# One pass over the edge tiles in layer 0's messages, with two accumulating products a tile

## The chip, the core and the metric

The kernel runs on one core of a Trainium2 chip. Its engines are TensorE (PE; its weight loads are shown as PEld), VectorE (DVE), ScalarE (ACT), GpSimd (POOL) and SyncE (SP), each with its own queue of instructions, and 16 DMA engines. The metric is the device time of one execution in microseconds (us), as the median of several runs.

## What is computed

Two blocks of a network on a graph: 6250 nodes with 256 features, 100000 edges sorted by `dst`. The change lies in the first layer, a graph convolution with symmetric normalisation (cut to what matters; self-loops are added to the edges):

```python
deg = segment_sum(ew_sl, row_sl)
dinv = where(deg > 0, rsqrt(deg), 0.0)
norm = dinv[row_sl] * ew_sl * dinv[col_sl]
xw = h6_all @ W
msgs = xw[col_sl] * norm[:, None]
h7 = segment_sum(msgs, row_sl) + b
h = relu(h7 @ W1 + b1)
out = h @ W2 + b2
```

Here `row` is `src` and `col` is `dst`: each edge takes the row of its `dst` node, times its weight, and adds it to its `src` node. After this layer come a mixture of 8 experts, a relational graph layer with 8 relations over the same edges (gathered by `src`, summed by `dst`), and a mixture of 6 experts. The data are float32.

## The kernel before, in words

Nodes are cut into NT = 49 blocks of 128. The edges, in the order of `dst`, are C_ = 782 tiles of 128 edges. They are written as records (dst, src, weight, src*8+type) to `edge_table` in HBM. If the edges are found not to be sorted by block, the branch at L207 reorders them first; it is not taken with these data.

**Tiles by block.** A tile of edges can straddle two blocks of `dst`. `tile_list` (L241) makes a list in which such a tile stands once for each block that it touches: T = C_ + NT - 1 = 830 entries, padded to TL = 832, in Q = 7 columns of 128. An indirect DMA on POOL (L315) gathers the edge table in that order into `M`. `dloc` (L330) is the edge's dst relative to the entry's block; `mine` (L333, L334) marks the edges of the entry that belong to that block; `srcm` (L335) is src+1 for those and 0 for the others. `dloc` goes to HBM as `lane_rows` (L337). `to_edges` (L340) turns four of these arrays by PE transposes so that an entry's 128 edges lie on the partitions: `srcT`, `ewT`, `dlocT`, `idxT`. `blkd` holds each entry's block. The pool "edges", in which all this lies, is closed at L354, and the pool "keys" takes its side of the memory.

**Keys and degrees (L532 to L698).** From `srcT` each edge entry gets a place in the order by `src`: comparisons against 49 blocks (`eq`, L545), counts (`pcnt`), a running sum, and for each block two pairs of products and a predicated copy into `pos` (L597 to L604), between which `x_times_w` produces the layer's product xw tile by tile into HBM. `at` (L612) is the place; edges that are not the entry's own have none. Then the weighted degree: over chunks of DCH = 32 columns, DVE builds one comparison (`ohl`, L663) and three products (`we`, L671), and PE accumulates one small product for each column (L678). `dinv` is known at L697. These loops run over all 832 columns.

**Messages (L699 to L771).** xw is loaded into `acc` (49 blocks of 256 columns and one of zeros), and ACT scales each block by `dinv` (L729). Then for each group of 8 entries: SP loads `lane_rows` broadcast over the partitions (L714, three groups ahead), DVE compares it with the partition's number to make eight selection matrices `sT` (L751), and copies the src number into the end of the message (L753); and for each entry PE multiplies the matrix with the block of `acc` named by a register (L756), ACT scales by the weight (L759), and POOL scatters the 128 rows of 260 floats to their places in `msgs` in HBM (L762). Rows without a place are skipped. `sT` has three buffers, `msg` four groups, and `psum_mm` four banks, one for each `px`. SP also loads x into X in five pieces (L743, L745), to which DVE adds b2 (L749).

```python
ps = psum_mm(f"px{t0 + j}")
nc.tensor.matmul(
    ps[:, :D], sT[:, j, :], acc[:, bass.ds(blocks[j] * D, D)], start=True, stop=True
)
```

**Sums (L774 to L797)** read `msgs` back in the order of `src` and add each tile into `acc`. Layer 1 (`layer1`, L1366, with `aggregate`, L799) uses `dlocT`, `idxT` and `blkd`, and stands in an if with an else (L1413 to L1416).

The code is written in a framework that sets the waits between the engines and orders the instructions between two branches by their dependences, not strictly as written.

Of the kernel before, what the change touches and what calls it, by code (L numbers as in the profile page):

```python
# [20 lines left out]
D = 256  # L21
E = 100000
NT = 49
# [8 lines left out]
TH = TL // 2  # L32
NOWHERE = 127 + 128 * 1024
# [6 lines left out]
DCH = 32  # L40
# [12 lines left out]
def gnn_ffn_kernel(ctx: ExitStack, tc: tile.TileContext, a, out):  # L53
# [221 lines left out]

    turn_i = sp.tile([128, Q * 128], I32, name="turn_i")
# [45 lines left out]

    Mf = M.bitcast(F32)
    dloc = sp.tile([128, Q, 128], F32, name="dloc")
    srcm = sp.tile([128, Q, 128], F32, name="srcm")
    idxf = sp.tile([128, Q, 128], F32, name="idxf")
    mine = sp.tile([128, Q, 128], F32, name="mine")
    dlocb = sp.tile([128, Q, 128], BF16, name="dlocb")
# [3 lines left out]
    nc.scalar.copy(dlocb, dloc)  # L332
    nc.vector.tensor_scalar(mine, dloc, 0.0, None, op0=OP.is_ge)  # L333
    nc.vector.scalar_tensor_tensor(mine, dloc, 128.0, mine, op0=OP.is_lt, op1=OP.mult)  # L334
    nc.vector.scalar_tensor_tensor(srcm, M[:, :, :, 1], 1.0, mine, op0=OP.add, op1=OP.mult)  # L335
    lane_rows = dram.tile([Q * 128, 128], BF16, name="lane_rows")
    nc.sync.dma_start(lane_rows.rearrange("(q p) e -> p q e", p=128), dlocb)  # L337


    def to_edges(name, pool, rows, dt):  # L340
        t = pool.tile([128, Q * 128], dt, name=name)
        for q0 in range(0, Q, 4):
            n = min(4, Q - q0)
            pt = psum_mm(f"p_{name}{q0}")
            for q in range(n):
                nc.tensor.transpose(pt[:, q * 128 : (q + 1) * 128], rows(q0 + q), ident)
            nc.scalar.copy(t[:, q0 * 128 : (q0 + n) * 128], pt[:, : n * 128])
        return t

    srcT = to_edges("srcT", g0p, lambda q: srcm[:, q], F32)  # L350
    ewT = to_edges("ewT", g0p, lambda q: Mf[:, q, :, 2], F32)
    dlocT = to_edges("dlocT", ed, lambda q: dloc[:, q], F32)
    idxT = to_edges("idxT", ed, lambda q: idxf[:, q], I32)
# [180 lines left out]
    srcT_i = kp.tile([128, TL], I32, name="srcT_i", tag="t1")  # L534
    nc.vector.tensor_scalar(srcT_i, srcT[:, :TL], -1.0, None, op0=OP.add)
    key_i = kp.tile([128, TL], I32, name="key_i", tag="t2")
    nc.vector.tensor_scalar(key_i, srcT_i, 7, None, op0=OP.arith_shift_right)
    hib = kp.tile([128, TL], BF16, name="hib")
    nc.vector.tensor_copy(hib, key_i)
    nc.vector.tensor_scalar(key_i, srcT_i, 127, None, op0=OP.bitwise_and)  # L540
    lob = kp.tile([128, TL], BF16, name="lob")
    nc.vector.tensor_copy(lob, key_i)
    eq = kp.tile([128, NT, TL], BF16, name="eq")
# [7 lines left out]
    for b in range(NT):  # L551
        for h in range(2):
            nc.tensor.matmul(
                pcnt[h][:NT, :TH],
                sel[:, NT - 1 - b : 2 * NT - 1 - b],
                eq[:, b, h * TH : (h + 1) * TH],
                start=(b == 0),
                stop=(b == NT - 1),
            )
    cnts = kp.tile([NT, TL], F32, name="cnts", tag="t1")  # L560
    for h in range(2):
        nc.scalar.copy(cnts[:, h * TH : (h + 1) * TH], pcnt[h][:NT, :TH])
    base = kp.tile([NT, TL], F32, name="base", tag="t3")
    one = ones[:NT, 0:1].to_broadcast([NT, TL])
    nc.vector.tensor_tensor_scan(base, one, cnts, 0.0, op0=OP.mult, op1=OP.add)
    tots = kp.tile([NT, 1], F32, name="tots")
    nc.vector.tensor_copy(tots, base[:, TL - 1 :])
# [12 lines left out]
    base_i = kp.tile([NT, TL], I32, name="base_i", tag="t2")  # L580
    nc.vector.scalar_tensor_tensor(base_i, base, start0, cnts, op0=OP.add, op1=OP.subtract)
    qr = kp.tile([64 + NT, TL], F16, name="qr")
    nc.vector.memset(qr, 0.0)
    half_i = kp.tile([NT, TL], I32, name="half_i", tag="t4")
# [10 lines left out]
    pos = kp.tile([128, TL], F32, name="pos", tag="t3")  # L595
    nc.vector.memset(pos, float(NOWHERE))
    for b in range(NT):  # L597
        for h in range(2):
            cs = slice(h * TH, (h + 1) * TH)
            pp = psum_mm(f"ppos{b}_{h}")  # L600
            nc.tensor.matmul(pp[:, :TH], beforeb, eq[:, b, cs], start=True, stop=False)
            nc.tensor.matmul(pp[:, :TH], selq[:, b : b + 1].to_broadcast([64 + NT, 128]), qr[:, cs], start=False, stop=True)
            nc.vector.copy_predicated(pos[:, cs], eq[:, b, cs].bitcast(U16), pp[:, :TH])
        next(xws, None)  # L604

    place = kp.tile([128, TL], I32, name="place", tag="t1")
    nc.vector.tensor_copy(place, pos)
    slot = kp.tile([128, TL], I32, name="slot", tag="t2")
    nc.vector.tensor_scalar(slot, place, 7, None, op0=OP.arith_shift_right)
    nc.vector.tensor_scalar(place, place, 127, None, op0=OP.bitwise_and)  # L610
    at = g0p.tile([128, TL], I32, name="at")
# [3 lines left out]
    past_s = kp.tile([NT, TL], F32, name="past_s", tag="t4")  # L615
# [32 lines left out]
    parts = kp.tile([128, 3, TL], BF16, name="parts")  # L648
    rest = kp.tile([128, TL], F32, name="rest", tag="t1")
    nc.vector.tensor_copy(parts[:, 0], ewT[:, :TL])  # L650
    nc.vector.tensor_sub(rest, ewT[:, :TL], parts[:, 0])
# [8 lines left out]
    for c0 in range(0, TL, DCH):  # L660
# [16 lines left out]
        for c in range(DCH):  # L677
# [5 lines left out]
                stop=(c0 + c == TL - 1),  # L683
# [24 lines left out]
    expand = ctx.enter_context(ExitStack())  # L708
    xp = expand.enter_context(tc.tile_pool(name="expand", bufs=3))

    def lanes_of(t0):

        rows = xp.tile([128, 8, 128], BF16, name=f"rows{t0}", tag="rows")
        nc.sync.dma_start(  # L714
            rows,
            lane_rows[t0 : t0 + 8, :].rearrange("(o t) e -> o t e", o=1).to_broadcast([128, 8, 128]),
        )
        return rows

# [14 lines left out]
    for t0 in range(0, TL, 8):  # L734
# [3 lines left out]
        if t0 + 24 < TL:  # L738
            ahead.append(lanes_of(t0 + 24))
# [733 lines left out]
```

## Time and profile before

| | us |
|---|---|
| median of 3 runs | 4283.4 (4282.7 to 4290.7) |
| the profiled execution | 4289.8 |
| its span, first to last instruction | 4288.1 |
| start to the last degree product | 0 to 384.6 |
| acc loaded and scaled | 386.3 to 414.4 |
| messages, first to last scatter | 416.5 to 1501.6 |
| sums, first read to the last product of the loop | 1503.2 to about 2000 |
| experts of layer 0, table of layer 1 | to 2943 |
| layer 1 with its experts | 2950 to the end |

```profile
span 4288.1 us, 48381 instructions
...
PE 3382.5 (79%) x12377; PEld 2237.3 (52%) x12377; DVE 1945.9 (45%) x5379; ACT 1016.3 (24%) x2275; POOL 2131.5 (50%) x2341
...
PE   2886555556555389997859959998789999999999
...
POOL 1000777777777755553740071003766666666640
PEclk9998777676776699998869979997889999999999
```

The last three rows cut the span into 40 slices of 107 us; a digit is the busy share in tenths, and for PEclk the share of its full clock that TensorE was granted. The messages are slices 5 to 14, counted from 1: POOL at 7, PE at 5 or 6, the clock at 6 or 7. A float32 product shows as two MATMUL rows.

### The profile page before, as it was taken

To read this page: it belongs to the slowest core of one execution; us is meant where nothing else is said; L and a number is where in the kernel's file an instruction comes from. 1 tells how busy PE (TensorE), PEld (TensorE's weight loads), DVE (VectorE), ACT (ScalarE), POOL (GpSimd) and SP (SyncE) were. 2 spreads that over 40 slices of the span, in tenths; PEclk is the share of its full clock that TensorE was granted. 3 is DMA by queue.
4 is the path that set the end of the run, shared out by engine and by line. 5 is a ranking of instruction groups with operands and counts; after the bars stand their busy time and mean duration, and the time that the engine had idled before them with its cause. 6 is when DMAs were issued, how large, how long until landed. Compare 5 with 4: busy or idle time off the path is not lost.

```text
span 4288.1 us, 48381 instructions
## 1 busy us (share of the span) xinstructions
PE 3382.5 (79%) x12377; PEld 2237.3 (52%) x12377; DVE 1945.9 (45%) x5379; ACT 1016.3 (24%) x2275; POOL 2131.5 (50%) x2341
## 2 busy tenths in 40 slices
PE   2886555556555389997859959998789999999999
PEld 1565444444444245554647724444556666666666
DVE  6686100000001078886743354333556566555552
ACT  3312333333333200000624411221111221212113
POOL 1000777777777755553740071003766666666640
PEclk9998777676776699998869979997889999999999
DMA  5514433333333266665233353333333333333320
GB/s 171 153 38 136 133 126 122 123 119 123 120 123 122 101 223 229 229 229 192 74 122 108 106 181 145 128 128 117 101 86 96 94 95 100 95 97 96 92 75 9
DMA packets 222105, 531.42 MB, mean 124 GB/s; under 512 B 44269, under 2 KB 128482, under 8 KB 201859
## 3 DMA queue, kind: packets, MB, share of 16 engines
q0 software_dynamic: 89648, 240.41, 17.6%
q1 hardware_dynamic: 105200, 209.11, 15.0%
q10 hardware_dynamic: 26976, 78.69, 5.3%
q8 instruction: 111, 1.82, 0.2%
q14 instruction: 170, 1.39, 0.1%
HBM read 317.07 MB, written 217.49 MB: 125 GB/s over the span
## 4 chain that ended last, share of the span: by engine, by line
PE 47%; DVE 6%; DMA 4%; POOL 3%; issue 3%; ACT 1%; DVEq 0%; SPq 0%; ACTq 0%; POOLq 0%
PE pa1a L820 7%; PE phx L1242 7%; PE pa L795 6%; PE ph_e1a L426 6%; PE py1a L899 5%; PE ph_e2a L426 5%; POOL m L793 2%; PE pf L1179 2%; PE pf L1195 2%; DMA y<-ys,ats 2%; DVE acc L797 2%; PE pt_fh L414 1%; DVE acc L822 1%; PE plo L1256 1%; PE pg L984 1%
## 5 line engine op out<-in xcount | busy, mean ns | idle before, releaser
L813 POOL DMA_INDIRECT g1a<-hx,idxT x830 | 800.8, 965 | 764.8 <-issue 399.1
L762 POOL DMA_INDIRECT msgs<-msg,at x830 | 832.4, 1003 | 598.9 <-DMA X<-in_x 346.2
L756 PE MATMUL px<-acc,sT 128*128 x1660 | 606.9, 544 | 475.5 <-ACT msg L759 442.6
L756 PEld LDWEIGHTS px<-acc,sT 128*128 128x128 f32 x1660 | 463.4, 286 | 618.3 <-ACT msg L759 482.4
L822 DVE TENSOR_TENSOR acc<-acc,pa1a 128x256 f32 x830 | 348.2, 420 | 392.8 <-PE pa1a L820 364.9
L759 ACT ACTIVATE msg<-px,ewT 128x256 f32<-128x256 f32 x830 | 357.6, 475 | 695.6 <-DMA msgs<-msg,at 566.4
L795 PE MATMUL pa<-g,m 128*128 128x256 f32 x1660 | 448.6, 419 | 84.4 <-DVE m L785 44.5
L820 PE MATMUL pa1a<-g1a,m1a 128*128 128x256 f32 x1660 | 480.2, 405 | 26.8 <-DMA g1a<-hx,idxT 12.3
L820 PEld LDWEIGHTS pa1a<-g1a,m1a 128*128 128x128 f32 x1660 | 318.3, 199 | 224.3 <-issue 147.8
L795 PEld LDWEIGHTS pa<-g,m 128*128 128x128 f32 x1660 | 250.7, 189 | 282.7 <-issue 115.8
L1242 PE MATMUL phx<-wr,xT 128*128 128x512 f32 x784 | 364.6, 619 | 36.0 <-DVE hx L1250 29.3
L797 DVE TENSOR_TENSOR acc<-acc,pa 128x256 f32 x830 | 348.4, 420 | 73.8 <-PE pa L795 5.9
L793 POOL TENSOR_SCALAR m<-lanes,key 128x128 f32<-128x128 f32 x414 | 263.8, 652 | 228.7 <-PE pa L795 205.7
L753 DVE COPY msg<-srcT 128x32 f32<-128x32 f32 x104 | 18.9, 183 | 696.2 <-DMA msgs<-msg,at 696.0
L899 PE MATMUL py1a<-w_L_ffn_expert_w,v2a 128*128 128x256 f32 x1176 | 284.1, 382 | 4.8 <-DVE acc L822 2.2
L426 PE MATMUL ph_e1a<-xT3a,w_L_ffn_expert_w 128*128 128x512 f32 (+2 forms) x672 | 284.8, 549 | 0.2 <-DVE acc L822 0.2
L426 PE MATMUL ph_e2a<-v1a,w_L_ffn_expert_w 128*128 128x512 f32 (+2 forms) x672 | 279.7, 542 | 2.6 <-DVE acc L822 2.2
L1242 PEld LDWEIGHTS phx<-wr,xT 128*128 128x128 f32 x784 | 152.3, 198 | 219.5 <-issue 181.9
L1219 POOL DMA_INDIRECT y<-ys,ats x98 | 96.7, 986 | 303.8 <-DMA w_L_ffn_expert_w<-in_L_ffn_expert_w 274.2
L899 PEld LDWEIGHTS py1a<-w_L_ffn_expert_w,v2a 128*128 128x128 f32 x1176 | 220.4, 190 | 43.8 <-ACT v2a L433 8.7
L433 ACT ACTIVATE v1a<-ph_e1a,cols 128x512 f32<-128x512 f32 (+2 forms) x168 | 106.5, 634 | 575.9 <-PE ph_e1a L426 575.8
L900 DVE SCALAR_TENSOR_TENSOR X<-py1a,C1a,X 128x256 f32<-128x256 f32 x294 | 139.2, 482 | 126.3 <-PE py1a L899 125.6
(606 smaller groups left out, 3756.6 us busy)
## 6 DMA issues: line engine op xcount, KB each, us to landing
g<-msgs SPq DMA_DIRECT2D x52, 1040.0 KB
g<-msgs ACTq DMA_DIRECT2D x52, 1040.0 KB, 4.9
hx<-hx SPq DMA_DIRECT2D x49, 1024.0 KB, 3.8
rows<-lane_rows SPq DMA_DIRECT2D x104, 256.0 KB, 3.6
fx<-xs SPq DMA_DIRECT2D x105, 128.0 KB, 2.0
ys<-fy ACTq DMA_DIRECT2D x105, 128.0 KB
msgs<-msg,at POOLq DMA_INDIRECT x830, 2.5
g1a<-hx,idxT POOLq DMA_INDIRECT x830, 2.8
```

What stands on the lines that cost most here:

```text
L426: nc.tensor.matmul(ps[:, :ncols], w[:, k, f * 128 : (f + 1) * 128], xT[:, k, :ncols], start=(k == 0), stop=(k == 1),)
L756: nc.tensor.matmul(ps[:, :D], sT[:, j, :], acc[:, bass.ds(blocks[j] * D, D)], start=True, stop=True)
L759: nc.scalar.activation(msg[:, j, :D], ps[:, :D], AF.Copy, scale=ewT[:, t0 + j : t0 + j + 1])
L762: ins = nc.gpsimd.indirect_dma_start(out=msgs, out_offset=bass.IndirectOffsetOnAxis(ap=at[:, t0 + j : t0 + j + 1], axis=0), in_=msg[:, j, ...
L793: nc.gpsimd.tensor_scalar(m[:, j], lanes, key[:, j : j + 1], None, op0=OP.is_equal)
L795: nc.tensor.matmul(ps[:, :D], m[:, j, :], g[:, j, :D], start=True, stop=True)
L797: nc.vector.tensor_add(here, here, ps[:, :D])
L813: nc.gpsimd.indirect_dma_start(out=g, out_offset=None, in_=table, in_offset=bass.IndirectOffsetOnAxis(ap=idxT[:, t0 + j : t0 + j + 1], axi ...
L820: nc.tensor.matmul(ps[:, :D], m[:, j, :], g, start=True, stop=True)
L822: nc.vector.tensor_add(here, here, ps[:, :D])
L899: nc.tensor.matmul(ps[:, :D], hT[:, k, j : j + 128], w[:, k, :], start=(k == 0), stop=(k == 1))
L1242: nc.tensor.matmul(ps, xT[:, k, :], wr[:, k, 2 * i : 2 * i + 2, :].rearrange("p r o -> p (r o)"), start=(k == 0), stop=(k == 1),)
```

## The change

The list of edge tiles that the messages use is now the natural one: each of the 782 tiles once (TN = 784 columns). What a tile needs beside its first block is taken from the block after it. A new table `Mn` is loaded without an indirect DMA; `lane` is the edge's dst relative to the tile's first block, 0 to 255 for an edge of the first two. Two comparisons per group of tiles make one selection matrix for each of the two blocks, and two products accumulate in PSUM. Two tiles share one PSUM bank, half each. Keys, places and degrees run over 784 columns instead of 832, and the degree chunks are 28 columns instead of 32. The gathered list stays for layer 1 (`dlocT`, `idxT`, `blkd`), and the places in `msgs` and the sums keep their 830 entries.

If any real edge lies beyond the second block (`far`), a flag is set, and a branch chooses another form of the loop, in which each tile's rows come by an indirect DMA from a copy of the scaled xw in HBM. The loop with the two products stands in its else.

```diff
+TN = (C_ + 7) // 8 * 8
+QN = (C_ + 127) // 128
+NH = TN // 2
-DCH = 32
+DCH = 28
...
+    nc.sync.dma_start(
+        Mn[:, : QN - 1].rearrange("p q e r -> p q (e r)"), table[:whole].rearrange("(q p) x -> p q x", p=128)
+    )
...
+    nc.vector.tensor_scalar(firstb_i, Mn[:, :, 0, 0], 7, None, op0=OP.arith_shift_right)
...
+    nc.vector.tensor_scalar(real, Mn[:, :, :, 0], float(NP), None, op0=OP.is_lt)
+    nc.vector.scalar_tensor_tensor(srcm, Mn[:, :, :, 1], 1.0, real, op0=OP.add, op1=OP.mult)
+    for q in range(QN):
+        nc.vector.tensor_scalar(lane[:, q], Mn[:, q, :, 0], firstn[:, q : q + 1], None, op0=OP.subtract)
+    nc.scalar.copy(laneb, lane)
...
+            nc.tensor.matmul(
+                pbn[:1, q * 128 : (q + 1) * 128], firstb[:, q0 + q : q0 + q + 1], ident, start=True, stop=True
+            )
...
+    nc.vector.tensor_mul(lane, lane, real)
+    nc.vector.tensor_reduce(far, lane, axis=AX.X, op=OP.max)
+    nc.vector.tensor_scalar(far, far, 256.0, None, op0=OP.is_ge)
...
-    nc.scalar.copy(dlocb, dloc)
-    nc.vector.tensor_scalar(mine, dloc, 0.0, None, op0=OP.is_ge)
-    nc.vector.scalar_tensor_tensor(mine, dloc, 128.0, mine, op0=OP.is_lt, op1=OP.mult)
-    nc.vector.scalar_tensor_tensor(srcm, M[:, :, :, 1], 1.0, mine, op0=OP.add, op1=OP.mult)
...
-    for t0 in range(0, TL, 8):
-        blocks = blocks_of(blkd, t0, [ENG.PE], NT)
+    def messages(tag, near):
...
+            for t0 in range(0, TN, 8):
+                n = min(8, C_ - t0)
...
-        sT = xp.tile([128, 8, 128], F32, name=f"sT{t0}", tag="sT")
-        nc.vector.tensor_scalar(sT, rows, part, None, op0=OP.is_equal)
+                if near:
+                    blocks = blocks_of(blkn, t0, [ENG.PE], NT - 1)
+                    sT = xp.tile([128, 2, 8, 128], F32, name=f"sT{tag}{t0}", tag="sT", bufs=2)
+                    for k in range(2):
+                        nc.vector.tensor_scalar(
+                            sT[:, k], rows, far_parts[:, k : k + 1], None, op0=OP.is_equal
+                        )
...
-            ps = psum_mm(f"px{t0 + j}")
-            nc.tensor.matmul(
-                ps[:, :D], sT[:, j, :], acc[:, bass.ds(blocks[j] * D, D)], start=True, stop=True
-            )
+                    if near:
+                        if j % 2 == 0:
+                            pair = psum_mm(f"px{tag}{t0 + j}")
+                        come = pair[:, j % 2 * D : (j % 2 + 1) * D]
+                        for k in range(2):
+                            nc.tensor.matmul(
+                                come,
+                                sT[:, k, j, :],
+                                acc[:, bass.ds(blocks[j] * D + k * D, D)],
+                                start=(k == 0),
+                                stop=(k == 1),
+                            )
+                    else:
+                        come = xp.tile([128, D], F32, name=f"come{tag}{t0 + j}", tag="come")
+                        nc.gpsimd.indirect_dma_start(
+                            out=come,
+                            out_offset=None,
+                            in_=xw,
+                            in_offset=bass.IndirectOffsetOnAxis(ap=to[:, j, 0:1], axis=0),
+                        )
...
+    nfar_v = nc.values_load(nfar[0:1, 0:1], min_val=0, max_val=128, skip_runtime_bounds_check_because="it is a count")
+    with tc.If(nfar_v > 0) as far_cmp:
+        messages("f", False)
+    with far_cmp.Else():
+        messages("n", True)
```

## The prediction

> **What bounds the kernel now.** I read the page's table of costliest groups first: the change sits in the message loop (L733 to L771), and three rows of that table are its engines.
>
> ```profile
> L762 POOL DMA_INDIRECT msgs<-msg,at x830 | 832.4, 1003 | 598.9 <-DMA X<-in_x 346.2
> ...
> L756 PE MATMUL px<-acc,sT 128*128 x1660 | 606.9, 544 | 475.5 <-ACT msg L759 442.6
> ...
> L759 ACT ACTIVATE msg<-px,ewT 128x256 f32<-128x256 f32 x830 | 357.6, 475 | 695.6 <-DMA msgs<-msg,at 566.4
> ```
>
> The columns after the bar are busy us, mean ns of one, idle us before and who ended it. ACT waits for scatters to land, PE waits for ACT: both run behind POOL. Then the timeline, at the start of the loop and in its middle (start, duration, idle before in brackets):
>
> ```profile
> 414.54 3.75 PE L756 MATMUL px<-acc,sT 128*128 x8 [30.01 <-DMA X<-in_x]
> 415.77 0.47 ACT L759 ACTIVATE msg<-px,ewT 128x256 f32<-128x256 f32 x1 [1.33 <-PE px L756]
> 416.52 1.02 POOL L762 DMA_INDIRECT msgs<-msg,at  x1 [346.20 <-DMA X<-in_x]
> ...
> 902.56 0.47 ACT L759 ACTIVATE msg<-px,ewT 128x256 f32<-128x256 f32 x1 [0.38 <-PE px L756]
> 903.41 0.47 ACT L759 ACTIVATE msg<-px,ewT 128x256 f32<-128x256 f32 x1 [0.38 <-PE px L756]
> ...
> 905.36 0.98 POOL L762 DMA_INDIRECT msgs<-msg,at  x1 [0.30 <-issue]
> 906.64 0.98 POOL L762 DMA_INDIRECT msgs<-msg,at  x1 [0.30 <-DMA msgs<-msg,at]
> ...
> 910.51 1.10 POOL L762 DMA_INDIRECT msgs<-msg,at  x1 [0.30 <-DMA msgs<-msg,at]
> ...
> 910.73 0.75 DVE L751 TENSOR_SCALAR sT<-rows,part 128x1024 f32<-128x1024 bf16 x1
> ```
>
> POOL issues a scatter every 0.98 + 0.305 = 1.285 us, and the 0.30 gap is the same whoever is named as releaser: POOL is saturated. 830 of them are 1066.6 us; the loop took 1085 (416.5 to 1501.6). The other 19 us are scatters longer than 0.98, nearly all ones that run beside an L751 compare, as at 910.51: it ends when the compare ends, plus 0.12.
>
> Before the loop, DVE bounds the degree loop (L660 to L683), a chunk every 4.86 us:
>
> ```profile
> 370.09 2.31 DVE L663 TENSOR_TENSOR ohl<-lob,lanes_b 128x4096 bf16<-128x4096 bf16 x1
> 372.29 2.76 DVE L671 TENSOR_TENSOR we<-parts,eq 128x1568 bf16<-128x1568 bf16 x3
> 374.94 2.31 DVE L663 TENSOR_TENSOR ohl<-lob,lanes_b 128x4096 bf16<-128x4096 bf16 x1
> ```
>
> **The change part by part.**
>
> *Scatters.* 830 become 782: 48 x 1.285 = **-61.7 us**, if POOL stays the bound.
>
> *Second compare.* L751 (0.75 us, x104) becomes two, x98 groups. DVE has room (9.4 busy us of 100 in the loop), but POOL pays: from 460 us on, the excess is 16.2 us over some 98 groups, 0.165 us per compare. One more per group: 98 x 0.165 = **+16 us**. Bounds: 4 (both compares fall under one scatter) to 40 (one that starts late in a scatter made it 1.29 to 1.49).
>
> *Second product.* PE's trace rows must be read with the clock, in the windows view (busy us of PE, PEld, DVE, ACT, POOL; granted clock; DMA share, GB/s):
>
> ```profile
> 414.00:420.00 6.00, 5.46 (x13) 4.42 (x14) 2.68 (x5) 2.81 (x7) 2.87 (x3) 0.51 1.09 349
> 420.00:434.00 14.00, 11.23 (x52) 9.38 (x51) 8.75 (x16) 11.71 (x27) 10.95 (x11) 0.98 1.00 346
> 900.00:1000.00 100.00, 58.58 (x157) 44.89 (x158) 9.39 (x19) 34.50 (x80) 76.62 (x77) 0.74 0.36 120
> 2970.00:2990.00 20.00, 18.02 (x32) 7.92 (x32) 8.89 (x18) 0.00 (x0) 15.12 (x17) 0.50 0.36 104
> ```
>
> At half clock a product (two MATMUL rows) comes every 0.855 us (902.56 to 903.41); at full clock 27 evictions followed in 11.71 us, 0.434 each. A tile of two products is therefore 1.71 cold and 0.87 warm, against POOL's 1.285. Were PE free to run ahead it would fit in either mix: a group of eight, begun cold, takes 3.4 + 5.2 = 8.6 us of POOL's 10.5.
>
> Two rules of the Trainium skill bear on it. First, two tiles now share one bank (`pair`), and "PSUM — Partial Sum Buffer", section "PSUM bank collisions raise a hardware error", says that PE may not write a bank while ACT reads any part of it: guard by bank, not by address. The trace cannot show this, since today each px has a bank of its own. By the rows alone a warm tile costs PE 0.87. By the rule the odd tile waits for the even tile's eviction: 0.87 + 0.21 (pxw: 148.36 + 0.85, its copy starts 149.42) + 0.474 + 0.06 to 0.15 (eviction ends 900.72, PE starts 900.78) + 0.87 = 2.48 to 2.57 a pair, 1.24 to 1.29 a tile. I take the rule's sum. It is just under POOL's 1.285 + 0.04, so POOL keeps the bound, without slack; ACT's four msg buffers (24 tiles ahead) absorb jitter. Cold, the same chain is 1.71 + 0.375 + 0.474 + 0.1 + 1.71 = 4.37 a pair, **2.19 a tile**.
>
> So the clock decides. "TensorE: Matmul & The Clock Gate", section "Why this matters for your kernels", asks only that PE have no idle gap over some 3 us. Our gaps would be under 1 us, so by the rule the chain is warm and costs nothing. The last row above disagrees: there layer 1's sums issue a product every 1.25 us, gaps under 1 us, and the clock stays at 0.50 for 54 us. I therefore took the clock's steps (every 3.41 us) and PE's share of streaming in each, worked out from the matmuls' starts: of 199 cold windows (414 to 1560 and 2945 to 3045 us) those up to 0.77 stayed cold and those above went warm; of 163 warm windows those under about 0.40 went cold. Layer 1's share is 0.855/1.25 = 0.68, stuck. The new cold chain is 3.42/4.37 = 0.78 on average, and with one gap of 0.95 drifting through windows of 3.41 it lies between 0.72 and 1.0, so one of the first two or three windows passes. Warm it is 0.65, far over 0.40, and stays. I take warm: 0 us on the path after the start.
>
> *The branch.* The loop moves into an else. Its value comes from the edge table, long before. SP, POOL, DVE and PE reach it while ACT still scales acc (to 414.4), so only ACT's entry counts: register load 0.29 and branch 0.05 (L1412 and L1413), and then the first instruction, for which the nearest row is layer 1's else:
>
> ```profile
> 2946.82 1.23 DVE L805 TENSOR_TENSOR m1a<-lanes,dlocT 128x1024 f32<-128x1024 f32 x1 [2.85 <-issue]
> ```
>
> That is 3.2 us: ACT is ready at 417.8 instead of 415.77, +2.0. Three tiles come at the cold 2.19 instead of 1.3: +2.7. Sum **+4.7 us**; bounds +1 (code already there) to +10. The upper end has SP's order: its three lane-row loads, today ahead of acc's (384.6), come behind them, near 406, and behind their bytes; the four X loads of 1.5 MB follow as now. Leaving: **+1.2 us**, as DVE's last instruction at 48.44 let POOL go on at 49.63 around L207; bounds 0 to 3.
>
> *Keys and degrees* go from 832 to 784 columns. From the two sizes above, DVE pays 0.546 ns per element: a chunk saves 512 x 0.546 + 3 x 196 x 0.546 ns = 0.60, 4.26 instead of 4.86; 28 x 4.26 - 26 x 4.86 = -7.1. The last chunk's matmuls (4.57) lose four: -0.5. L601/L602: 4 matmuls of 24 fewer columns, 10 ns each at full clock, x49 = -2. eq and the scan chain: -0.8. Sum **-10 us**; bounds -6 to -12 (any interleaving with PE hides some).
>
> *The natural table.* Added on DVE: seven subtractions (0.33, as L330) 2.3, `real` 0.6, the mask and maximum 2.0, casts and memset 2.4; gone `mine` 1.7; srcm moves. Net +5.6 us, of which most finds the 17 us that DVE idles between 60 and 107. SP loads 1.8 MB more, 5 us at the 350 GB/s seen at 420, ahead of the xa loads. The keys no longer need the gather, but their pool lies where the edge pool lay, which closes only after idxT (86.4), so nothing comes earlier for certain. **+3 us**, between -5 and +8. The seven blkn products use an idle PE.
>
> The sums that follow (L774 on) still handle 830 tiles and are untouched.
>
> **Sum**: -61.7 + 16 + 4.7 + 1.2 - 10 + 3 = **-46.8**. The profiled execution took 4289.8 (span 4288.1), giving 4243; the median of the runs is 4283.4, 6.4 lower, and the forecast is for a median: **4237 us**. All costs at their low ends give -61.7 + 4 + 1 + 0 - 12 - 5 = -74 (4210); at their high ends -61.7 + 40 + 10 + 3 - 6 + 8 = -7 (4277).
>
> **The rivals.**
>
> *A cold chain (slower).* The bank hand-over at L756/L759 holds PE at half clock as in layer 1. A cold tile is 2.19 instead of POOL's 1.325, so each costs 0.865; -46.8 is eaten by 54 such tiles, 118 us of cold clock. Half the tiles cold: 391 x 0.865 = +338, **4575 us**. For it: 54 us stuck at 2949, and 0.78 against a threshold of 0.77. Against: drifting windows, and the warm chain's wide margin over 0.40. 9%.
>
> *Compare for free.* Back-to-back compares hit the same scatter, or PE's order spreads them: the +16 becomes +4, entry +1, table 0: -67, **4216 us**. For it: 563 of the 798 scatters after 460 us take 0.985 or less. Against: compares beside a scatter lengthen it again and again. 22%, largely within the range.
>
> *Warm chain a little slower than POOL*: 1.36 to 1.40 a tile from latencies I did not count: 782 x 1.38 = 1079, -6 in the loop and -1 outside, **4276 us**. 10%.
>
> *The far branch is taken.* Two indirect DMAs a tile, 782 x 2.57 = 2010: 4283 + 924 = **5207 us**. A node has 16 edges, a block 2048, a tile 128, so none reaches a third block. 1%.
>
> The likeliest case has 58%. Range 4209 to 4277 leaves out the cold chain, the far branch and the ends of others. About 0.2% (8.6 us) is what runs of this kernel can tell from no change: faster 0.85, same 0.05, slower 0.10.
>
> **What would show it.** L762 x782 with a median of 0.98, gaps 0.30, mean near 1.02, and a loop of 1040 us; L751's successor x196; PE rows x3128 and PEclk 9 or 10 in its slices; ACT's idle time still ended by landing scatters. Degree chunks every 4.3 us, 28 of them. A loop over 1085, POOL waiting for ACT, and PEclk 5 would mean the cold chain. Wrong also if the first scatter comes later than about 415, or the sums begin later than 4 us after the last scatter.

## The result

The changed kernel takes **4222.1 us** (median; 4221.8 to 4224.5) against 4284.9 for the kernel before in the same set: ratio 0.9853, 95% interval 0.9836 to 0.9870. In a second set it was 4218.9 against 4287.2: 0.9843 (0.9826 to 0.9859). The forecast was 4237; the fall is 62.8 and 68.3 us, where the prediction worked out 46.8. Direction and range held; the sum was 16 and 21.5 us short, and which of its terms were is the matter of what follows.

The page of the changed kernel, costliest groups, for the three engines of the message loop:

```profile
L844 POOL DMA_INDIRECT msgs<-msgn,at x782 | 793.1, 1014 | 554.2 <-DMA M<-edge_table,natq_i 316.1
L826 PE MATMUL pxn<-acc,sTn 128*128 x3128 | 794.4, 414 | 243.6 <-DVE sTn L807 217.1
...
L841 ACT ACTIVATE msgn<-pxn,ewT 128x256 f32<-128x256 f32 x782 | 370.1, 473 | 642.6 <-PE pxn L826 472.8
```

782 scatters instead of 830, and their mean went from 1003 to 1014 ns. PE makes nearly twice as many products, yet its mean row fell from 544 to 414 ns, since the clock rose. The windows view (PE, PEld, DVE, ACT, POOL busy; clock; DMA share, GB/s) says so by stage:

```profile
402.00:408.00 6.00, 5.80 (x18) 4.79 (x19) 1.86 (x4) 1.57 (x4) 1.69 (x2) 0.64 1.07 363
420.00:434.00 14.00, 12.67 (x57) 9.86 (x55) 5.83 (x10) 7.10 (x15) 10.95 (x11) 1.00 0.69 219
900.00:1000.00 100.00, 75.93 (x301) 58.32 (x299) 14.42 (x29) 35.98 (x76) 76.83 (x77) 0.93 0.39 126
2881.00:2901.00 20.00, 14.23 (x25) 6.24 (x26) 7.23 (x14) 0.00 (x0) 15.07 (x15) 0.50 0.33 93
```

PE starts cold, is at full clock 4 us later and stays near it (0.93, against 0.74 before); layer 1's sums still sit at 0.50. POOL does the same work per 100 us as before (77 scatters). One group in the middle of the loop, in the timeline:

```profile
904.77 1.11 POOL L844 DMA_INDIRECT msgs<-msgn,at  x1 [0.31 <-DMA msgs<-msgn,at]
904.86 0.18 DVE L817 COPY msgn<-srcT 128x32 f32<-128x32 f32 x1 [8.99 <-DMA msgs<-msgn,at]
905.00 1.42 DVE L807 TENSOR_SCALAR sTn<-rowsn,far_parts 128x1024 f32<-128x1024 bf16 x2
905.81 7.42 PE L826 MATMUL pxn<-acc,sTn 128*128 x32 [3.12 <-DVE sTn L807]
906.18 1.08 POOL L844 DMA_INDIRECT msgs<-msgn,at  x1 [0.30 <-DMA msgs<-msgn,at]
...
909.82 0.47 ACT L841 ACTIVATE msgn<-pxn,ewT 128x256 f32<-128x256 f32 x1 [0.39 <-PE pxn L826]
910.68 0.47 ACT L841 ACTIVATE msgn<-pxn,ewT 128x256 f32<-128x256 f32 x1 [0.39 <-PE pxn L826]
```

All 781 gaps between POOL's scatters are still 0.30 us (the largest is 0.31), so POOL is still the bound. PE does a group in 7.4 us and then waits 3.1 for DVE, whose copy waits for scatters to land. Evictions (ACT's copies of a tile out of PSUM) are 0.86 us apart: a tile of two products takes the 0.87 that the rows alone gave, not the chain's 1.24 to 1.29. Two scatters in each group of eight are longer than 0.98: those beside the two compares.

Where the time went, in the two profiled executions (spans 4288.1 and 4219.6, together -68.4):

| stretch | before | after | change | forecast |
|---|---|---|---|---|
| start to the degree sums (copy to degs) | 384.6 | 376.4 | -8.1 | -7 (table +3, keys and degrees -10) |
| degree sums to first scatter | 32.0 | 29.6 | -2.4 | +4.7 |
| first scatter to end of last | 1085.1 | 1031.2 | -53.9 | -45.7 (-61.7 + 16) |
| last scatter to first key | 9.05 | 9.39 | +0.3 | +1.2 |
| first key to end | 2777.4 | 2773.0 | -4.4 | 0 |

The degree loop is as forecast, a chunk every 4.29 us:

```profile
359.41 2.01 DVE L706 TENSOR_TENSOR ohl<-lob,lanes_b 128x3584 bf16<-128x3584 bf16 x1
361.35 2.43 DVE L714 TENSOR_TENSOR we<-parts,eq 128x1372 bf16<-128x1372 bf16 x3
363.70 2.01 DVE L706 TENSOR_TENSOR ohl<-lob,lanes_b 128x3584 bf16<-128x3584 bf16 x1
```

### The profile page after: what moved, and what is told of

It is laid out like the page before. It is cut to its first block, busy times and chain, and to the rows that moved or that the text cites. A ratio compares the mean times of both kernels' runs of the same rounds, so it can differ in the third digit from the quotient of the medians.

```text
span 4219.6 us, 51857 instructions
## 1 busy us (share of the span) xinstructions
PE 3555.7 (84%) x13813; PEld 2379.1 (56%) x13813; DVE 1988.8 (47%) x5492; ACT 1027.7 (24%) x2227; POOL 2090.9 (50%) x2293
## 4 chain that ended last, share of the span: by engine, by line
PE 47%; DVE 8%; DMA 3%; issue 3%; POOL 3%; ACT 1%; DVEq 1%; SPq 0%; PEldq 0%; ACTq 0%; POOLq 0%
PE pa1a L907 8%; PE phx L1329 7%; PE ph_e1a L469 6%; PE py1a L986 5%; PE ph_e2a L469 5%; PE pa L882 5%; DVE acc L884 3%; PE pf L1266 2%; PE pf L1282 2%; POOL m L880 2%; DMA y<-ys,ats 2%; DVE acc L909 1%; PE pg L1071 1%; PE pt_fh L457 1%; PE plo L1343 1%
## 5 line engine op out<-in xcount | busy, mean ns | idle before, releaser
L844 POOL DMA_INDIRECT msgs<-msgn,at x782 | 793.1, 1014 | 554.2 <-DMA M<-edge_table,natq_i 316.1
L826 PE MATMUL pxn<-acc,sTn 128*128 x3128 | 794.4, 414 | 243.6 <-DVE sTn L807 217.1
L826 PEld LDWEIGHTS pxn<-acc,sTn 128*128 128x128 f32 x3128 | 616.0, 207 | 421.9 <-DVE sTn L807 284.3
L841 ACT ACTIVATE msgn<-pxn,ewT 128x256 f32<-128x256 f32 x782 | 370.1, 473 | 642.6 <-PE pxn L826 472.8
L907 PE MATMUL pa1a<-g1a,m1a 128*128 128x256 f32 x1660 | 476.3, 402 | 31.2 <-DMA g1a<-hx,idxT 12.5
L817 DVE COPY msgn<-srcT 128x32 f32<-128x32 f32 x98 | 18.0, 186 | 834.9 <-DMA msgs<-msgn,at 703.2
```

The lines of the kernel that those rows point to most:

```text
L826: nc.tensor.matmul(come, sT[:, k, j, :], acc[:, bass.ds(blocks[j] * D + k * D, D)], start=(k == 0), stop=(k == 1),)
L841: nc.scalar.activation(msg[:, j, :D], come, AF.Copy, scale=ewT[:, t0 + j : t0 + j + 1])
L844: ins = nc.gpsimd.indirect_dma_start(out=msgs, out_offset=bass.IndirectOffsetOnAxis(ap=at[:, t0 + j : t0 + j + 1], axis=0), in_=msg[:, j, ...
L907: nc.tensor.matmul(ps[:, :D], m[:, j, :], g, start=True, stop=True)
```

## The experiments

They ran in three sets, each on one chip. On the chip of the first set the kernel before takes 4540 us, on the others 4287 and 4290. Totals are therefore compared within a set; times up to the first scatter can be read in all of them.

| kernel | us | before, same set | ratio (95%) | degs | first scatter | loop | scatters' excess over 0.98 |
|---|---|---|---|---|---|---|---|
| own_bank | 4488.9 | 4540.0 | 0.9888 (0.9872 to 0.9905) | 373.2 | 402.6 | 1156.9 | 30.5 |
| no_branch | 4500.2 | 4540.0 | 0.9903 (0.9886 to 0.9919) | 378.7 | 406.6 | 1173.6 | 25.5 |
| natural_late | 4493.8 | 4540.0 | 0.9891 (0.9874 to 0.9908) | 367.6 | 398.0 | 1171.4 | 22.2 |
| one_product | 4456.9 | 4540.0 | 0.9812 (0.9795 to 0.9828) | 372.1 | 402.9 | 1129.3 | 21.8 |
| after_again | 4218.9 | 4287.2 | 0.9843 (0.9826 to 0.9859) | 372.5 | 403.3 | 1031.2 | 26.7 |
| rows_first | 4220.4 | 4287.2 | 0.9847 (0.9830 to 0.9863) | 374.1 | 406.1 | 1023.7 | 18.9 |
| third_compare | 4217.5 | 4287.2 | 0.9836 (0.9820 to 0.9853) | 373.8 | 404.3 | 1031.5 | 27.0 |
| extra_scatters | 4287.5 | 4287.2 | 1.0001 (0.9992 to 1.0010) | 373.2 | 404.0 | 1098.2 | 30.8 |
| natural_late_2 | 4218.7 | 4289.9 | 0.9836 (0.9822 to 0.9849) | 369.7 | 400.6 | 1032.7 | 28.2 |
| own_bank_2 | 4219.5 | 4289.9 | 0.9837 (0.9822 to 0.9852) | 374.6 | 404.3 | 1031.4 | 26.9 |
| one_product_2 | 4211.3 | 4289.9 | 0.9820 (0.9805 to 0.9835) | 372.4 | 402.9 | 1023.1 | 19.0 |
| one_bank | 5256.4 | 4289.9 | 1.2256 (1.2237 to 1.2274) | 372.9 | 403.7 | 2067.2 | 53.8 |

after_again is the changed kernel once more; what each of the others changes stands in its section. "degs" is the start of the copy to degs (L732), "loop" first scatter to end of the last; the excess adds up what each scatter lasted over 0.98 us.

### The price of a scatter

> The changed kernel itself, as the reference for the other runs of this set, since an earlier set ran on a chip on which the kernel before takes 4540 us. Where the kernel before takes 4284 it takes 4222 again, with a loop (first scatter to end of the last) of 1031 and a stretch from the first key of the sums to the end of 2773, which the profile of before had 4.4 longer: if that is chance, it will vary by some us here too. Where the kernel before takes 4540, POOL waits for messages, the loop takes about 1160, and the total is about 4490.

It took 4218.9, and its loop and excess are those of the first profile to 0.1 us. It reaches the degree sums 4 us sooner (372.5 against 376.4): this much varies between two profiles of one kernel before the loop.

```diff
+    spill = dram.tile([128 * TS, RW], F32, name="spill")
...
+                    if near and j == 0 and t0 % 16 == 0:
+                        ins = nc.gpsimd.indirect_dma_start(
+                            out=spill,
...
+                            in_=msg[:, 0, :],
```

> The changed kernel with 49 scatters more: the first tile of every second group is also written, at the same places, to a second buffer in DRAM that nobody reads. It measures the price of a scatter by itself. Forecast and trace agree on 1.285 us where POOL is the bound: the loop grows by 63 us, the total by 63 against the changed kernel on the same chip. If the bound is not POOL, or the DMA rings are, the loop grows by clearly less or more.

The loop grew by 67.0 us and the total by 68.6, 4 to 5 above the 63 forecast. The page's row for the added ones says why:

```profile
L856 POOL DMA_INDIRECT spill<-msgn,at x49 | 55.6, 1135 | 14.9 <-DMA msgs<-msgn,at 12.5 <-issue 2.1 <-DMA M<-edge_table,natq_i 0.3
```

They last 1.135 each, because they stand where the compares run, while the others fell from 1014 to 1010 ns: 49 x (1.135 + 0.305) - 782 x 0.0045 = 67.0. So the loop is POOL's instructions end to end, and the 48 scatters that the change saves are most of the gain (61.7 of the 68.4 us): 49 more bring the time back to that of the kernel before.

### One, two and three compares

```diff
-                    for k in range(2):
+                    for k in range(1):
                         nc.vector.tensor_scalar(
                             sT[:, k], rows, far_parts[:, k : k + 1], None, op0=OP.is_equal
...
-                        for k in range(2):
+                        for k in range(1):
                             nc.tensor.matmul(
```

> The changed kernel with the first block alone compared and multiplied (the part of the messages that comes from the second block is left out), where POOL is the bound. Forecast: a compare costs POOL 0.165 us, so the scatters' sum over 0.98 falls by 16 us (27 to 11). Theory after the run with three compares, which cost no more than two: what stretches scatters is a block of DVE work that begins inside one and still runs when the next begins; one compare of 0.75 us stretches one scatter by 0.11 instead of two, so the sum falls by 10 (27 to 17), the loop to 1021, the total to 4210. If the second product cost something, the loop would fall further, though POOL can't go below 1005.

```diff
+                    sX = xp.tile([128, 8, 128], F32, name=f"sX{tag}{t0}", tag="sX", bufs=1)
+                    nc.vector.tensor_scalar(sX, rows, far_parts[:, 0:1], None, op0=OP.is_equal)
```

> The changed kernel with a third compare in each group, whose result nobody reads. Forecast: 0.165 us of POOL for each compare, +16 us in the sum of the scatters' times over 0.98 (27 to 43). By the trace after (two compares cost 7.5 more than one): +7.5, to 34. If the three run back to back (2.1 us) they cover two scatters as two compares do, and only their sum grows.

The excess is 19.0 with one compare, 26.7 with two and 27.0 with three. The second costs 7.7 us, less than the 10 that the newer theory gave, and the third 0.3. (The run with one compare leaves out the second product as well. Its loop is 8.1 to 8.3 us shorter, 7.7 of it in the excess, so the second product costs the loop 0.6 us at most.) The forecast's price per compare (16 us for the second, and as much for a third) falls. The timelines, first with one compare, then with three:

```profile
907.91 1.11 POOL L844 DMA_INDIRECT msgs<-msgn,at  x1 [0.30 <-DMA msgs<-msgn,at]
...
908.15 0.75 DVE L807 TENSOR_SCALAR sTn<-rowsn,far_parts 128x1024 f32<-128x1024 bf16 x1
...
909.33 0.99 POOL L844 DMA_INDIRECT msgs<-msgn,at  x1 [0.30 <-DMA msgs<-msgn,at]
```

```profile
904.25 1.09 POOL L846 DMA_INDIRECT msgs<-msgn,at  x1 [0.31 <-ACT msgn L843]
...
904.47 0.75 DVE L811 TENSOR_SCALAR sXn<-rowsn,far_parts 128x1024 f32<-128x1024 bf16 x1
...
905.13 1.41 DVE L807 TENSOR_SCALAR sTn<-rowsn,far_parts 128x1024 f32<-128x1024 bf16 x2
905.65 1.10 POOL L846 DMA_INDIRECT msgs<-msgn,at  x1 [0.30 <-DMA msgs<-msgn,at]
```

One compare stretches the scatter in which it begins, to 1.11, and that ends 0.12 after the compare; the next is free. Two reach into the next scatter, which takes 1.08. Three cover that second scatter almost whole (to 906.54 of 906.75), and it takes 1.10 all the same. So in these three runs a stretched scatter costs 0.1, whether 0.24 us of compare lie in it or nearly 0.9; the number of scatters touched counts, not the compares. By place in the group of eight, after 460 us, the mean excess of the second and third scatter is 0.123 and 0.109 us with two compares, 0.125 and 0.009 with one, 0.098 and 0.105 with three; all others are under 0.011.

What the first of them costs depends on when the compare begins. In rows_first (next section), which has two compares, they begin 0.14 us (median) after the scatter instead of 0.24; the scatter again ends 0.12 after the first compare, and takes 1.01:

```profile
912.45 1.01 POOL L844 DMA_INDIRECT msgs<-msgn,at  x1 [0.30 <-DMA msgs<-msgn,at]
912.58 1.42 DVE L807 TENSOR_SCALAR sTn<-rows,far_parts 128x1024 f32<-128x1024 bf16 x2
```

The next one costs 0.11 there as well, and the whole excess is 18.9, no more than with one compare. In the kernel before, where nine in ten compares began 0.16 to 0.82 us after a scatter, 132 of the 798 scatters after 460 us lie beside one, 1.4 for each compare, and carry 14.0 of the 16.2 us: 0.11 each. The wrong step of the forecast was to divide the excess by the number of compares, and to charge a compare that follows another without a break like one that stands alone.

### The way to the first scatter

```diff
-    nfar_v = nc.values_load(nfar[0:1, 0:1], min_val=0, max_val=128, skip_runtime_bounds_check_because="it is a count")
-    with tc.If(nfar_v > 0) as far_cmp:
-        messages("f", False)
-    with far_cmp.Else():
-        messages("n", True)
+    messages("n", True)
```

> The changed kernel with the near loop in line: no branch, the far form is left out. The forecast put entry at +4.7 us and leaving at +1.2: without the branch the first scatter would follow the end of the scaling (402) by about 2 us instead of 3.9, and the total would be 4216. The theory formed from the trace after: the branch is also a boundary that keeps the loop's first loads and compares out of the chain that makes dinv; in line they slip back into it, dinv comes some 8 us after the degree sums instead of 3.6, the first scatter about 32 us after them instead of 29.6, and the total is 4222 to 4226, no gain.

Against the kernel with a bank for every tile, which has the branch and ran in the same set, the first scatter followed the degree sums after 27.9 us instead of 29.4. Of these 1.5 us (1.5 to 2.9 against all profiles with it, 29.4 to 30.9) the scaling has a part: it lasts 19.7 in line and 20.3 to 20.6 with the branch, but 20.3 in line in the kernel before too, which no run explains. From the end of the scaling to the first scatter it is 3.0 in line and 3.7 to 5.2 with the branch, so entering it costs 0.7 to 2.3 us. The theory that the branch keeps the loop's compares out of dinv's chain falls: in line, the scaling starts 5.2 us after the sums, with it 5.1 to 5.4. The total rose all the same, since the degree sums came 5.5 us later here and the loop was longer; the compiled order of the instructions ahead of the loop differs too, so the totals of these two don't price the branch.

What differs from the kernel before must then be the place of the first three row loads. The change moved them behind acc's. This run puts them back, in the kernel of no_branch:

```diff
+    expand = ExitStack()
+    xp = expand.enter_context(tc.tile_pool(name="expand", bufs=3))
...
+    ahead = [lanes_of(t0) for t0 in (0, 8, 16)]
     nc.vector.memset(acc[:, NT * D :], 0.0)
     for t in range(0, NT, 7):
         nc.sync.dma_start(
             acc[:, t * D : (t + 7) * D].rearrange("p (t d) -> p t d", d=D),
```

> The near loop in line, and its first three loads of lane rows ahead of acc's loads in the program, as in the kernel before. It puts a cause to the forecast's missing +7 us between the degree sums and the first scatter. Theory: what kept the chain that makes dinv short is that the change moved these loads behind acc's: with them ahead, the compares of the first groups stand between dinv's steps on DVE and wait for their rows, so acc's scaling starts 8 to 10 us after the degree sums instead of 5.3, and the first scatter comes 31 to 33 us after them, against 27.9 in line with the loads behind. Rival: the order of the loads doesn't matter and the scaling starts 5.3 us after the sums here too.

The scaling starts 9.4 us after the sums and the first scatter 32.0, as in the kernel before (9.6 and 32.0). So the order of the loads is the cause, but not by the way that the theory named. SP's queue in the kernel before (degs at 384.57):

```profile
384.56 1.28 SPq L714 DMA_DIRECT2D rows<-lane_rows  x3
386.27 16.04 SPq L723 DMA_DIRECT2D acc<-xw  x7
```

SP's, DVE's and ACT's timelines in this run, then in the changed kernel (degs at 374.07 and 376.44):

```profile
374.06 1.29 SPq L756 DMA_DIRECT2D rows<-lane_rows  x3
375.60 15.00 SPq L765 DMA_DIRECT2D acc<-xw  x7
...
377.48 0.75 DVE L807 TENSOR_SCALAR sTn<-rows,far_parts 128x1024 f32<-128x1024 bf16 x1 [1.40 <-DMA rows<-lane_rows]
378.15 0.46 DVE L415 RECIPROCAL deg_r<-deg_h 128x49 f32<-128x49 f32 x1
378.52 0.65 DVE L807 TENSOR_SCALAR sTn<-rows,far_parts 128x1024 f32<-128x1024 bf16 x1
...
381.11 0.21 DVE L740 TENSOR_TENSOR deg_o<-deg_o,some 128x49 f32<-128x49 f32 x1
...
383.46 0.91 ACT L771 ACTIVATE acc<-acc,deg_o 128x256 f32<-128x256 f32 x2 [7.10 <-DMA acc<-xw]
```

```profile
376.44 13.07 SPq L753 DMA_DIRECT2D acc<-xw  x7
...
378.42 0.47 DVE L415 RECIPROCAL deg_r<-deg_h 128x49 f32<-128x49 f32 x1 [0.31 <-ACT deg_h L414]
...
379.87 0.21 DVE L740 TENSOR_TENSOR deg_o<-deg_o,some 128x49 f32<-128x49 f32 x1
...
381.78 11.33 ACT L759 ACTIVATE acc<-acc,deg_o 128x256 f32<-128x256 f32 x28 [3.40 <-DMA acc<-xw]
```

With the rows first, compares that wait for them do stand between dinv's steps, and dinv's last step (L740) ends 7.3 us after the sums instead of 3.6. But ACT goes on waiting for 2.1 us more, and the bracket says for what: acc's first load to land, in both kernels. That load is issued 1.5 us after the sums instead of at once, behind three row loads on SP's queue, and it lands 7.9 us after its issue (383.46 - 375.60) instead of 5.3, which fits the rows' 3 x 256 KB ahead of it: 2.2 us at the 350 GB/s of the forecast's first window (an estimate). 1.5 + 2.5 is the 4.0 by which the scaling is later; the first scatter differs by 4.1 between the two in-line kernels (32.0 and 27.9), which ran on different chips. How much would be left with the loads behind and the compares still in the chain wasn't tried. This loop is 7.5 us shorter, since its compares begin earlier in a scatter (above). The total shows none of it (4220.4): the first scatter came 2.8 later and the stretch from the first key on took 2775.2 instead of 2770.0.

### PE, the shared bank and the clock

```diff
-                        if j % 2 == 0:
-                            pair = psum_mm(f"px{tag}{t0 + j}")
-                        come = pair[:, j % 2 * D : (j % 2 + 1) * D]
+                        pair = psum_mm(f"px{tag}{t0 + j}")
+                        come = pair[:, :D]
```

> The changed kernel with a PSUM bank for every tile, where POOL is the bound. If the hand-over of a shared bank is hidden by the order of PE's products, evictions stay 0.86 us apart in the middle of a group in both, POOL's gaps stay 0.30, and the total is within 4 us of 4220. If it costs what the forecast's chain says, the changed kernel would have shown it in the burst; here the burst shortens and the total is the same.

4219.5 and a loop of 1031.4, as with shared banks; evictions are 0.86 apart, and PE's group took 7.31 us instead of 7.42. The compiled order of PE in the changed kernel shows why (each tile has two products; pxn104 and pxn106 are two banks of one group):

```
pxn104  tile 0, first half of bank A    waits DVE
pxn106  tile 2, first half of bank B
pxn104  tile 1, second half of bank A   waits ACT
pxn106  tile 3, second half of bank B   waits ACT
```

The trace agrees: of the eight tiles of a group the third, fourth, seventh and eighth in PE's order wait for ACT. The wait that the bank rule of "PSUM — Partial Sum Buffer" asks for is there, but tile 2 stands between the two tiles of bank A, and its 0.87 us cover the forecast's 0.74 to 0.83 of latency, eviction and restart (0.21 + 0.474 + 0.06 to 0.15). The hand-over uncovered is the next run:

```diff
-                        if j % 2 == 0:
+                        if t0 + j == 0:
                             pair = psum_mm(f"px{tag}{t0 + j}")
-                        come = pair[:, j % 2 * D : (j % 2 + 1) * D]
+                        come = pair[:, :D]
```

> The changed kernel with a single PSUM bank for all tiles, so that every tile's products wait for the eviction of the tile before and nothing can stand between: the chain of the forecast, uncovered. With its terms a warm tile takes 0.87 + 0.21 + 0.474 + 0.1 = 1.65 us, and PE is the bound: loop 1290, total 4480. Cold it is 1.71 + 0.375 + 0.474 + 0.1 = 2.66 with a share of streaming of 0.64, under the 0.77 that took windows to full clock: by the forecast's thresholds PE starts cold and stays cold, loop 2080, total 5270. By the page's rule of a gap over some 3 us it warms and stays warm, since no gap is over 1 us: 4480.

5256.4 us, loop 2067. Timeline and two windows:

```profile
1001.28 2.08 PE L826 MATMUL pxn<-acc,sTn 128*128 x4 [0.56 <-ACT msgn L841]
1001.50 0.98 POOL L844 DMA_INDIRECT msgs<-msgn,at  x1 [1.66 <-ACT msgn L841]
1003.39 0.47 ACT L841 ACTIVATE msgn<-pxn,ewT 128x256 f32<-128x256 f32 x1 [2.17 <-PE pxn L826]
1003.92 2.07 PE L826 MATMUL pxn<-acc,sTn 128*128 x4 [0.57 <-ACT msgn L841]
```

```profile
420.00:500.00 80.00, 63.02 (x123) 35.85 (x122) 10.35 (x19) 14.20 (x30) 31.23 (x31) 0.50 0.20 65
900.00:1100.00 200.00, 156.66 (x303) 88.87 (x303) 15.74 (x29) 35.97 (x76) 79.19 (x76) 0.50 0.18 62
```

A tile every 2.64 us (1003.92 - 1001.28), where the forecast's terms gave 2.66, and half clock for the whole of the loop. No gap of PE in it was over 0.615 us. So short gaps alone did not bring the array to full clock: at a share of streaming of 1.71 / 2.64 = 0.65 it stayed cold for 2067 us. The changed kernel, from the same cold start, was at full clock 4 us after its first product (402.2 to 406.3).

The forecast had taken more from the Trainium skill than stands there. In "TensorE: Matmul & The Clock Gate", section "Why this matters for your kernels", the row on gaps is about falling from full clock; another row of the table, on reaching it, asks that TensorE be busy for 4 us or more without a break, and this chain idles 0.56 us before every tile. The run agrees with that row; the 4480 "by the page's rule" came from the wrong one. The traces ask for less than "without a break", though.

The 0.77 that the forecast read from the trace before holds in the changed kernel's loop too. With 0.427 us of streaming counted from the start of each MATMUL row at half clock, the clock stayed down after 14 of the 56 windows (3.41 us each) at half clock, all with a share of 0.776 or less, and rose after 42, all with 0.785 or more; in the single-bank run no window is over 0.73. It decides here between the estimated 4480 and the measured 5256. The forecast's other limit, about 0.40 for falling from full clock, comes out somewhat lower in the same count: windows fell up to 0.35 in the kernel before and up to 0.39 in the changed one.

> The changed kernel with a PSUM bank for every tile instead of one for two tiles. The forecast's chain (the odd tile's products wait for the even tile's eviction, 1.24 to 1.29 us a tile) says that PE's burst for a group of eight shortens from some 10 us to 7.0 (8 x 0.87). The theory formed from the trace after says that the bank is handed over for nothing, since PE puts the neighbouring pair's even tile between the two tiles of a bank: evictions stay 0.86 to 0.87 us apart, the burst stays 7.0 to 7.5 us, and the total stays at 4222, within 4 us either way. By both POOL keeps the bound, so the burst decides, not the total.

> The changed kernel with only the first block compared and multiplied (the part of the messages that comes from the second block is left out). It isolates the second compare and the second product. Forecast: the compare costs POOL 16 us, so the loop (first scatter to end of the last) falls from 1031 to 1015 and the total to 4206. By the trace after it costs 7.5: loop 1024, total 4215. If the second product cost something on the path, the loop would fall to the floor of 782 x 1.285 = 1005 or the total by more than 20 us. PE falls to half clock for most of the loop (share of streaming 0.34 warm), without effect.

On the chip of the first set neither question could be put as meant, because POOL is not the bound there:

```profile
709.65 1.52 POOL L843 DMA_INDIRECT msgs<-msgn,at  x1 [1.84 <-DVE sTn L807]
```

This is one of 141 gaps over 0.35 us in the kernel with a bank for every tile, ended by DVE or by ACT; ACT ran ahead of POOL by 2.6 us (median), against 18.0 in the changed kernel's profile. There the second compare and product together cost some 28 us of loop (1156.9 to 1129.3; the two kernels also differ in their banks). The stretch from the first key to the end was longer there too (2912 to 2920 against 2769 to 2775). What is slower on that chip was not settled.

### The natural table

The block from `Mn` to `nfar` was moved behind the gather of `M`, unchanged:

```diff
-    Mn = sp.tile([128, QN, 128, 4], I32, name="Mn")
...
-    nc.vector.tensor_copy(nfar, nfar_f)
...
             in_offset=bass.IndirectOffsetOnAxis(ap=natq_i[:, q : q + 1], axis=0),
         )
...
+    Mn = sp.tile([128, QN, 128, 4], I32, name="Mn")
...
+    nc.vector.tensor_copy(nfar, nfar_f)
```

> The changed kernel with the whole natural-table block behind the gather of the tile list in the program. Theory: the block's DVE work ahead of the tile list delayed the gather by 20 us and the start of the key positions by 6; moved behind, the gather starts near 62 again, the positions start near 141, and the total falls by 5 to 6 us to 4216. Rival: the positions are bound by PE and by the normalisation that runs beside them, not by their start, so what is gained early is lost there: 4220 to 4224.

> The changed kernel with the natural-table block behind the gather, once more: the first time it ran on a chip that takes 4540 us for the kernel before, where its first scatter came at 398.0 against 402.6 for the changed kernel with a bank for every tile. Theory: on a chip that takes 4284 for the kernel before, the first scatter comes 4 to 6 us before the changed kernel's (403.3 and 406.0 in two profiles), the loop stays at 1031, and the total is 4213 to 4217 against 4219 to 4222. Rival: nothing of it is left at the end, 4219 to 4222.

The theory held up to the first scatter: 398.0 against 402.6 in the first set, 400.6 against 402.9 to 404.3 in the last. At the end nothing of it can be told: 4493.8 against 4488.9 in the first set, and in the last 4218.7 against 4219.5 for the kernel with a bank for every tile, whose loop was 1.3 shorter and whose end came 2.0 sooner after the first key. It is no better version that a measurement can show.

## Why the forecast was right, and where it fell short

**Scatters, -61.7.** Right: gaps of 0.305 throughout, and 49 more scatters cost 67.0 of loop.

**Second compare, +16.** The mechanism was right, the size wrong: 7.7 us. "0.165 us per compare" is really some 0.11 for each scatter that a compare touches, and in the kernel before a compare touched 1.4 of them. The second compare, back to back with the first, touches one more in each group: 98 x 0.10 (0.109 - 0.009) = 9.8, of which 1.8 are hidden because the other six scatters of a group are 3 ns longer in the run with one compare. This is 8 of the 22 us that the sum lacks against the profiled executions.

**Second product, 0.** Right in the sum, by a wrong chain, and so in part by luck. The odd tile's 1.24 to 1.29 never occurred, because PE's order puts another bank's tile between. Of the clock argument the limit of 0.77 was tested, at 2.64 us a tile, and held. The call that the forecast's own cold chain, at 0.78, would get warm was not tested, since that chain never ran.

**Branch entry, +4.7.** This step failed: the stretch became 2.4 us shorter in the first profile, 1.1 to 2.5 in all. It has three parts. From the sums to the start of the scaling, 9.58 became 5.34, which is -4.2: the prediction named the move of the row loads behind acc's as a risk only ("The upper end has SP's order"), and it was a gain, since in the kernel before those loads held back acc's, and with them the scaling. The scaling is 0.1 longer. From its end to the first scatter, 2.1 became 3.9 (3.7 to 5.2 in all), +1.8 where 4.7 was forecast: ACT's entry and the cold tiles were added up, but they run side by side. ACT's first eviction begins 3.1 us after the scaling, and PE had by then been done with that tile for 1.0 us:

```profile
405.25 0.47 ACT L841 ACTIVATE msgn<-pxn,ewT 128x256 f32<-128x256 f32 x1 [3.10 <-PE pxn L826]
```

Later cold tiles cost POOL nothing (no gap over 0.31). In line, where ACT enters nothing, the cold products do show: ACT waits 2.2 us for the first, and POOL 1.19 before its second scatter (no_branch). This step is some 7 us of the missing 22.

**Leaving, +1.2.** Measured 0 to +0.4 (9.0 to 9.4 against 9.05; 9.0 in line).

**Keys and degrees -10, table +3.** Their sum is near: -8.1 in the first profile, -10 to -12.5 in the later ones that have the table where the change has it, but -5.9 in no_branch, whose instructions ahead of the loop stand in another order. In parts it was +6.2 at the end of eq (123.9 to 130.1), and -14.3 from there to the sums: both were taken too small, and that they cancel is luck.

**Downstream, 0.** First key to end took 2769.0 to 2774.7 in eight profiles of kernels with the branch, outside the first set, 2777.4 before and 2775.2 in line. A spread of 5.7 where nothing behind the loop differs doesn't let -4.4 be put down to a cause, though all eight lie below the one profile before; it stays open. With 8 in the loop, 7 in the way to it, and 1 each at its end and before the sums it makes up the missing 22.

**The rivals.** "Compare for free" (4216) was the nearest, half for the reason given: compares share scatters, as three do, but two still stretch two. (Its -67 leaves out the 1.2 for leaving the branch; with it the sum is 4218.) The cold chain exists, as one_bank shows, but needs an uncovered hand-over. The chain "a little slower than POOL" didn't appear where the kernel before takes 4284 to 4290; on the slower chip something like it did.

## What to carry to other kernels

Where one engine issues without a gap, count its instructions first: the rest of a change is worth only what it adds to or takes from that engine's stream, and a run with some instructions added checks the price. Don't spread a loss from two engines running side by side over the operations that seem to cause it: vary their number (one, two, three), because what counts may be how many of the victim's instructions are touched, and at which point of them. When a loop moves into a branch or a function, follow its first loads too, and past which loads of the same queue they move: what is fetched ahead for the loop can hold back what the loop waits for first.

## What was not expected of the hardware

A third back-to-back compare of 0.75 us on DVE beside POOL's scatters cost 0.3 us in 98 groups, where the second cost 7.7. PE held half clock for 2067 us on end with no gap over 0.615 us. And the same kernel took 4540 us on one chip and 4287 and 4290 on two others, with the change worth 1.1% there (own_bank, whose total equals the changed kernel's elsewhere) and 1.5 to 1.6% here.
